# Layer 1's cross attention: the last keys' share moved within a turn, and the convolution's passes set apart

## The chip, the cores and the metric

The kernel runs on one core of one Trainium2 chip. The core has TensorE (PE, matmuls into PSUM), VectorE (DVE), ScalarE (ACT), GpSimd (POOL) and SyncE (SP, which issues most DMAs). Each engine works through its own queue in order and waits for the others by semaphores. The metric is device microseconds of one execution, the median of several runs.

## The reference, cut to what matters

Two layers work on `x` of 64 sequences x 32 places x 256 features. The change lies in layer 1, where a cross attention to 257 context rows per sequence (16 heads of 16 features) is followed by a gated mixer with a convolution over three places:

```python
x = x + xattn(layernorm(x), ctx, ctx, mask)      # 16 heads, 257 keys
...
xpad = jnp.pad(x, ((0, 0), (1, 1), (0, 0)))
t_out = xpad[:, :-2] * conv_w[:, 0] + xpad[:, 1:-1] * conv_w[:, 1] + xpad[:, 2:] * conv_w[:, 2]
return t_out + y_global
...
x = x + moe(layernorm(x))                        # 8 experts, 2 per token, 1 shared
```

All arithmetic is float32 but for a few exact bf16 operands. The output is the final `x`.

## The kernel before

The 2048 rows of `x` lie in four groups of four tiles of 128 rows; a tile is four sequences. Layer 0 runs first and ends near 240 us. Layer 1's cross attention runs from there to about 715 us, then the mixture of experts (`mixture`), with gathers, an expert loop and the final sum.

**Turns and steps.** `cross_attention` (L984) is a software pipeline: turn `i` of 18 handles three tiles at once, `after` (keys), `now` (scores and exponentials) and `before` (transposes and context), with `done` being projected. A turn has four steps `b`, one per sequence of the tile. The order of the work is written out by hand: every engine's queue follows the order of the Python calls. In one step PE sees: the first `ps_t` (four transposes of `before`'s weights), `ps_p` (the projection of `done`, in step 1 alone), `ps_v` (values), the second `ps_t`, the side work's matmuls, `ps_k` (keys), `ps_s` (scores), `ps_le` (step 1 alone) and `ps_o` (context).

DVE sees: the copy `eT` of the first `ps_t`, the reciprocal of the sums (`xsm`), in every second step the two `own` operations, in step 1 the add `x<-ps_p`, the copy `eT` of the second `ps_t`, the side work, and four minima (`CUSTOM_DVE_ANT_0 e<-ps_s,mask`, each with a short read of `xnm`). ACT takes the exponentials after the minima, and copies `v`, keys and transposes. POOL scales the exponentials (`e<-e,xsm`, four a step, after `last`), and does small and side work.

**The last key.** 257 is 256 + 1. The weights of the last key are gathered in `last` by POOL; `spread` (L1157, step 0) makes `lx` from them on POOL; `last_keys` (L1170, step 1) multiplies by a constant on PE (`ps_le`), by the last values on DVE (`lv<-ps_le,vl`) and adds the values' bias on POOL (`lv<-lv,vec`). `own_heads` (L1242), run one step after the context of steps 1 and 3, adds `ps_o` to `lv` on DVE and gives `own`, which `project` uses.

**Banks.** `ps_t` has one PSUM bank (b5), so the second `ps_t` of a step needs the first to be copied. Most of the rest (`ps_p`, `ps_v`, `ps_k`, `ps_le`, and all matmuls of side work) share a ring of two banks, b0 and b1, taken in turn in program order: a matmul waits until the reader of the one before the last is done.

**Side work.** Each step also takes a piece of a generator (`next(side)`, L1353). In turns 0 to 11 it is layer 0's linear part (`linear`: four rounding operations on `big`, `y` and `q` in steps 1 and 2 of turns 1, 5 and 9; two `ps_ff` in turns 2, 6 and 10), the normalisation and the queries of the next group. From turn 12 it is `late_pieces` (L957): mixers of four tiles for groups 0, 1 and 2, a mixer of two tiles for group 3, and three normalisations for the experts. A normalisation puts DVE's `st`, `mv`, `ve`, `half`, `r`, then fourteen small POOL operations (`sq`, `rn`, `off`), then `y` on ACT or DVE, and adds a bias row to `x` on POOL (`x<-x,rows`). `mixer` (L734) then gives `psT` (transposes), `ps_huv`, a scan `sums`, `hub`, `ps_g`, another `hub`, for each half `c` of the features `ps_d` and three passes of the convolution on DVE (`conv`; only the first reads `ps_d`), and `ps_x`, whose transposes bring `conv` back into `x`.

L120 is the line of all matmuls, L123 of all transposes, L108 of all DVE, ACT, POOL and SP operations. The functions below carry the changed lines.

## Time and profile before

| what | value |
|---|---|
| time, median of 3 runs | 962.22 us (961.95 to 964.1) |
| the profiled execution: its own time | 959.8 us |
| the profiled execution: its span | 958.0 us |
| mean granted clock of PE | 0.981 |
| PE busy in the span | 879.9 us (92%) |
| DVE, ACT, POOL busy | 606.9, 455.1, 541.4 us |
| PE busy from 620 to 645 us | 24.17 of 25 us |
| PE busy from 645 to 670 us | 17.93 of 25 us |
| PE busy from 670 to 695 us | 23.86 of 25 us |

Times in the profile are microseconds from the start of the span. A timeline's line has start, duration, engine, line, operation, output<-inputs and shape; in brackets stands the idle time of the engine just before it and who ended that. PE's ends are modelled, and successive matmuls overlap a little, so the text works with the distance from start to start.

### The profile page before, as it was taken

The page shows a single profiled execution, that of the slowest core. Times are in us where ns is not written, and L with a number is a line of the kernel's source. Part 1 is how long each engine was busy: PE and PEld are TensorE (multiplying, and loading weights), DVE is VectorE, ACT ScalarE, POOL GpSimd, SP SyncE. Part 2 cuts the span into 40 slices and gives each one's busy share as a digit, 9 for nine tenths or more (in the row PEclk, how much of TensorE's full clock was granted, in tenths as well). Part 3 has the DMA queues.
Part 4 walks back from the last instruction along what each step waited for, and adds up shares of the span by engine and source line. Part 5 has one row for each costly group of instructions (what it writes and reads, how often), then busy time and mean ns, then how long its engine had stood idle before and what let it go on. Part 6 is the DMA issues. An engine that isn't in the chain of part 4 may idle for free.

```text
span 958.0 us, 21439 instructions
## 1 busy us (share of the span) xinstructions
PE 879.9 (92%) x8005; PEld 607.9 (63%) x8035; DVE 606.9 (63%) x1734; ACT 455.1 (48%) x1163; POOL 541.4 (57%) x1056
## 2 busy tenths in 40 slices
PE   5899899888999999999999999997988999999991
PEld 3466666565456666566666665654757688888881
DVE  6889997797676677676777566877647722111116
ACT  3667677665455555454555466554532212222210
POOL 5779787893684656574755556647513045554420
PEclk9999999999999999999999999999999989999996
DMA  6753335343110111111111003000010337767617
GB/s 184 211 139 101 74 83 138 77 123 105 46 50 7 51 51 51 51 51 51 51 51 51 18 35 95 1 2 23 23 34 23 122 108 246 231 231 236 200 58 263
DMA packets 66073, 89.73 MB, mean 94 GB/s; under 512 B 31504, under 2 KB 49072, under 8 KB 63920
## 3 DMA queue, kind: packets, MB, share of 16 engines
q1 hardware_dynamic: 62128, 77.86, 26.5%
q0 software_dynamic: 3840, 10.49, 3.3%
q8 instruction: 64, 1.05, 0.5%
q14 instruction: 41, 0.34, 0.1%
HBM read 66.30 MB, written 13.63 MB: 83 GB/s over the span
## 4 chain that ended last, share of the span: by engine, by line
PE 50%; DVE 14%; POOL 14%; issue 10%; DMA 6%; ACT 4%; SPq 2%; POOLq 0%; ACTq 0%; DVEq 0%
PE ps_v L120 10%; PE ps_k L120 10%; PE ps_t L123 6%; PE ps_s L120 5%; PE ps_o L120 4%; POOL yg L108 4%; POOL r_rows L1721 3%; PE ps_p L120 3%; PE ps_qk L120 3%; PE ps_sh L120 3%; ACT e L108 3%; DMA r_rows<-og,lv 2%; SPq L108 2%; POOL sq L108 1%; PE ps_q L120 1%
## 5 line engine op out<-in xcount | busy, mean ns | idle before, releaser
L108 ACT ACTIVATE e<-e,xnm 128x257 f32<-128x257 f32 x256 | 127.8, 501 | 52.0 <-DVE xnm L108 46.0
L108 DVE CUSTOM_DVE_ANT_0 e<-ps_s,mask 128x257 f32<-128x257 f32 x256 | 93.4, 420 | 50.1 <-PE ps_s L120 49.3
L120 PE MATMUL ps_k<-ct,w_w_l1x 128*128 128x512 f32 x256 | 122.3, 600 | 1.6 <-ACT yT L108 0.6
L120 PE MATMUL ps_v<-w_w_l1x,ct 128*128 128x256 f32 x512 | 121.9, 381 | 0.0
L108 POOL TENSOR_SCALAR e<-e,xsm 128x256 f32<-128x256 f32 x256 | 121.1, 491 | 0.0
L123 PE MATMUL ps_t<-cst,e 128*128 128x128 f32 x640 | 100.5, 280 | 7.8 <-DVE eT L108 6.9
L108 DVE COPY eT<-ps_t 128x512 f32<-128x512 f32 x128 | 87.9, 687 | 26.8 <-PE ps_t L123 26.7
L120 PEld LDWEIGHTS ps_v<-w_w_l1x,ct 128*128 128x128 f32 x512 | 94.1, 192 | 11.0 <-issue 0.2
L123 PEld LDWEIGHTS ps_t<-cst,e 128*128 128x128 f32 x640 | 74.0, 141 | 35.5 <-issue 14.6
L108 POOL TENSOR_TENSOR x<-x,rows 128x256 f32<-128x256 f32 x96 | 70.5, 751 | 40.0 <-DVE y L108 17.0
L108 ACT ACTIVATE hTr<-ps_h,w 128x256 f32<-128x256 f32 x80 | 33.7, 472 | 124.9 <-issue 97.3
L108 ACT ACTIVATE kT<-ps_k,vec 128x512 f32<-128x512 f32 x64 | 44.2, 691 | 100.5 <-PE ps_k L120 100.3
L108 DVE TENSOR_TENSOR og<-ps_o,b 128x512 f32<-128x512 f32 x20 | 13.8, 690 | 116.0 <-PE ps_o L120 113.3
L1721 POOL DMA_INDIRECT r_rows<-og,lv x40 | 39.5, 987 | 70.2 <-DVE og L108 59.9
L108 ACT ACTIVATE kb<-kT,cst 128x256 f32<-128x256 f32 x160 | 70.9, 513 | 4.1 <-POOL kT L108 4.1
L120 PE MATMUL ps_h<-ygT,w 128*128 128x256 f32 x320 | 72.4, 379 | 0.0
L120 PE MATMUL ps_o<-w,hTr 128*128 128x256 f32 x320 | 72.2, 379 | 0.0
L120 PEld LDWEIGHTS ps_k<-ct,w_w_l1x 128*128 128x128 f32 x256 | 44.5, 190 | 41.6 <-issue 35.3
L120 PEld LDWEIGHTS ps_o<-w,hTr 128*128 128x128 f32 x320 | 60.8, 190 | 8.3
L108 ACT COPY v<-ps_v 128x512 f32<-128x512 f32 x80 | 46.7, 584 | 37.5 <-PE ps_v L120 37.1
L120 PEld LDWEIGHTS ps_h<-ygT,w 128*128 128x128 f32 x320 | 59.3, 190 | 7.3
L108 POOL TENSOR_TENSOR last<-e,xsm 128x4 f32<-128x4 f32 x64 | 12.9, 202 | 89.9 <-DVE xsm L108 89.9
(197 smaller groups left out, 1728.2 us busy)
## 6 DMA issues: line engine op xcount, KB each, us to landing
ct<-in_ctxT SPq DMA_DIRECT2D x16, 1024.0 KB
w<-in_ew SPq DMA_DIRECT2D x20, 514.0 KB
w<-in_ew SPq DMA_DIRECT2D x20, 512.0 KB
far<-part SPq DMA_DIRECT2D x64, 128.0 KB
v_rows<-v SPq DMA_DIRECT2D x16, 256.0 KB
vb<-v_rows SPq DMA_DIRECT2D x64, 64.0 KB
r<-r_rows SPq DMA_DIRECT2D x8, 512.0 KB
b<-in_eb SPq DMA_DIRECT2D x20, 128.0 KB
```

The lines of the kernel that those rows point to most:

```text
L108: ins = getattr(self.engine, name)(*args, **kw)
L120: return kept(nc.tensor.matmul(ps, **args))
L123: return kept(nc.tensor.transpose(ps, src, eye))
L1721: wrote = nc.gpsimd.indirect_dma_start(out=r_rows, out_offset=bass.IndirectOffsetOnAxis(ap=write_i[:, at : at + 1], axis=0), in_=o[:, i, : ...
```

## The change

`last_keys(before)` moves within step 1 from behind the scores to a place between the second `turned` and the side work. The second and third pass of the convolution are no longer issued at once: they are put in a list, `vector_later`, and `vector_steps` takes one of them out behind the scores of a step (behind the four minima, ahead of the next step's first `eT` copy) and one ahead of `values` and the second `turned` of a step (ahead of the second `eT` copy). In mixers of two tiles (`n == 2`) both are taken out at once.

```diff
+    vector_later = []
+
+    def vector_steps(n=1):
+        for _ in range(min(n, len(vector_later))):
+            vector_later.pop(0)()
+
...
             vector.scalar_tensor_tensor(got, yT[:, c, :], tap(1), ps, ALU.mult, ALU.add)
-            vector.scalar_tensor_tensor(
-                dst[:, :, 1:S], src[:, :, 0 : S - 1], tap(0), dst[:, :, 1:S], ALU.mult, ALU.add
-            )
-            vector.scalar_tensor_tensor(
-                dst[:, :, 0 : S - 1], src[:, :, 1:S], tap(2), dst[:, :, 0 : S - 1], ALU.mult, ALU.add
-            )
+            vector_later.append(
+                lambda dst=dst, src=src, by=tap(0): vector.scalar_tensor_tensor(
+                    dst[:, :, 1:S], src[:, :, 0 : S - 1], by, dst[:, :, 1:S], ALU.mult, ALU.add
+                )
+            )
+            vector_later.append(
+                lambda dst=dst, src=src, by=tap(2): vector.scalar_tensor_tensor(
+                    dst[:, :, 0 : S - 1], src[:, :, 1:S], by, dst[:, :, 0 : S - 1], ALU.mult, ALU.add
+                )
+            )
+            if n == 2:
+                vector_steps(2)
             conv.append(got)
...
                 if before is not None:
+                    vector_steps()
                     v = values(before, b)
                     turned(before, b, 1, eT)
                     if b == 0:
                         spread(before)
+                    if b == 1:
+                        last_keys(before)
                 next(side, None)
...
                     weights = scores(now, b)
+                vector_steps()
                 if before is not None:
-                    if b == 1:
-                        last_keys(before)
                     own_heads = context(before, b, eT, v)
```

## Prediction

> **What bounds the kernel now.** I read the page first, for the engine that sets the pace; then TensorE's waits between 240 and 715 us, where layer 1's attention runs; then the timelines of TensorE, VectorE and GpSimd around each wait.

> ```profile
> PE 879.9 (92%) x8005; PEld 607.9 (63%) x8035; DVE 606.9 (63%) x1734; ACT 455.1 (48%) x1163; POOL 541.4 (57%) x1056
> PE   5899899888999999999999999997988999999991
> PEclk9999999999999999999999999999999989999996
> ```

> TensorE (PE) is full in nearly every slice from the 11th to the 27th; the 28th (647 to 670 us) is not. So in the attention a change gains or loses only what it does to PE's own waits:

> ```profile
> PE ps_t L123 <- DVE eT L108: 6.9, 6, 2.9
> PE psT L123 <- DVE conv L108: 5.8, 5, 2.2
> PE ps_le L120 <- DVE hub L108: 0.7, 1, 0.7
> ```

> Total us, times, longest. All three end on VectorE (DVE): the copy of transposed weights (eT), the first convolution pass that empties the bank ps_d, and hub. Where the large ones stand, on PE:

> ```profile
> 389.12 0.66 PE L123 MATMUL ps_t<-cst,e 128*128 128x128 f32 x4 [0.86 <-DVE eT L108]
> ...
> 646.61 0.63 PE L123 MATMUL ps_t<-cst,e 128*128 128x128 f32 x4 [0.91 <-POOL rn L108]
> ...
> 649.11 1.12 PE L120 MATMUL ps_g<-hub,gw 64*128 64x512 f32 x2 [0.90 <-DVE x L108]
> ...
> 663.47 0.66 PE L123 MATMUL ps_t<-cst,e 128*128 128x128 f32 x4 [2.90 <-DVE eT L108]
> ...
> 667.50 0.66 PE L123 MATMUL psT<-cst,y 128*128 128x128 f32 x4 [2.07 <-DVE conv L108]
> ...
> 670.62 2.65 PE L120 MATMUL ps_v<-w_w_l1x,ct 128*128 128x256 f32 x8
> ...
> 696.68 0.66 PE L123 MATMUL psT<-cst,y 128*128 128x128 f32 x4 [2.20 <-DVE conv L108]
> 698.10 0.66 PE L123 MATMUL psT<-cst,y 128*128 128x128 f32 x4 [0.76 <-DVE conv L108]
> ```

> The reader is to see that 7.9 us of waits stand between 660 and 698. The reason is on DVE, in the same stretch:

> ```profile
> 657.29 2.12 DVE L108 SCALAR_TENSOR_TENSOR conv<-yT,vec,conv 128x496 f32<-128x496 f32 x2
> ...
> 662.40 0.42 DVE L108 TENSOR_TENSOR lv<-ps_le,vl 128x256 f32<-128x256 f32 x1
> 662.74 0.68 DVE L108 COPY eT<-ps_t 128x512 f32<-128x512 f32 x1
> ...
> 665.46 0.35 DVE L108 SCALAR_TENSOR_TENSOR own<-ps_o,cst,lv 128x128 f32<-128x128 f32 x1 [1.55 <-POOL lv L108]
> ...
> 694.91 0.35 DVE L108 SCALAR_TENSOR_TENSOR own<-ps_o,cst,lv 128x128 f32<-128x128 f32 x1 [2.86 <-POOL lv L108]
> ```

> and behind it on GpSimd (POOL):

> ```profile
> 661.19 0.19 POOL L108 TENSOR_TENSOR sq<-r 128x2 f32<-128x2 f32 x1 [0.51 <-DVE r L108]
> ...
> 664.81 0.61 POOL L108 TENSOR_TENSOR lv<-lv,vec 128x256 f32<-128x256 f32 x1
> ```

> Two convolution passes and lv hold up the eT copy. Then own waits for POOL's lv, which stood behind a normalisation's fourteen small steps (sq ... off), and the eT copy and the convolution's first pass queue behind own.

> **Part one: last_keys moves ahead of the side work.** Nothing is added; in 16 turns the ps_le matmuls (0.58 us from start to start), DVE's lv (0.42, the next instruction 0.34 later) and POOL's lv (0.61) move up. No DMA moves, so SP's queue is as before. On POOL, lv goes ahead of the bias adds and the sq steps, which start up to 0.6 us later; their readers on ScalarE come microseconds later. PE could now wait for POOL's lx: the tightest turn has lx done at 270.55, while the new place is at 271.30. Cost nothing; if that cover went, one turn would pay part of lx's 1.2 us.

> The banks do change. The ring has two: ps_p, ps_v, then ps_le takes the bank of ps_p and the next matmul that of ps_v. By the rows, x<-ps_p is done before that in 14 turns; in the two others (457 and 655 us) the same wait was already paid by the matmul that followed. ScalarE's copy of v ends about 0.85 us after the second ps_t starts; the new user comes at 1.01. Again nothing, with a cover of 0.1. The third user of the ring waits for lv.

> - Rounding turns (3: lv at 276, 381, 486). DVE has no gap between the eT copy and the minima, because of four rounding operations. lv now delays the minima by 0.38, then the exponentials, the reciprocal and the whole next step, where PE already waits (0.86 in the row at 389). 3 x 0.38 = +1.1.
> - Output turns of the linear layer (3: around 301, 406, 511). ps_k is the third user: its place is 299.65, lv ends at 299.85, release 0.06 later. 3 x 0.26 = +0.8.
> - Turns that transpose or normalise (8): the second psT waits 0.16 for lv, but ps_k waits anyway until ScalarE has emptied the first. The eT copy of the next step comes 0.2 later against a slack of 0.64 before PE needs it. 0.
> - The turn at 592: ps_le waits 0.68 for hub, as third user. Now ps_huv is second and nothing waits for hub until ps_v, at 593.75 against hub's new end of 593.27. -0.7.
> - The last two turns (657, 689): POOL's lv ends near 659 and 687 instead of 665.42 and 694.87, so own waits no longer. Counted below.

> **Part two: the passes.** Per channel half the first pass stays; the second goes behind the four minima and ahead of the next eT copy, the third ahead of the other eT copy. Six halves of three four-tile mixers are touched. In the two-tile mixers both passes run at once, in the old order: 0. A pass takes 0.74 us alone and 1.08 beside POOL's bias adds; I take 0.75 for the second and 0.75 to 0.95 for the third, which starts when POOL begins to scale e. Five on the path at the far ends would be 5 x 0.33 = 1.7, which goes into the range.

> - 604 to 623: minima waited for PE there (0.62 idle), so the passes were free; now the eT copy at 609.84 starts 0.75 late, PE pays 0.15. One turn on, the eT copy, lv and the transposes ps_x stand in a row and ps_g pays 0.34. +0.5.
> - 637: the eT copy is late by 0.1. +0.1.
> - 642 to 649: the worst place. The passes ran while DVE waited for ScalarE's hub (they ended at 641.07, the scan began at 641.23). Now the second stands between minima and eT copy: 0.72 on the wait of 0.91. The third follows own, at 648.45, and ps_x needs it: ps_g starts at 650.65 instead of 649.11. So with the two lines above PE is 1.5 late here. +0.9.
> - 655 to 663: without the two passes ahead (2.12) the minima start at 661.0 as before, though their inputs come 1.5 later. No lv, one pass: the eT copy ends at 663.9, PE goes on at 663.95. From 1.5 late to 0.5 late: -1.1.
> - 663 to 667.5: own does not wait (1.55), the third pass costs 0.75; the first pass of the other half ends at 666.75 instead of 667.45. From 0.5 late to 0.7 early: -1.2.
> - 667.5 to 675: the minima come 2.1 earlier. The granted clock reads 0.50 from 670 to 672 here: ps_o, ps_t and ps_v took 1.08, 1.12 and 2.65 us against 0.65, 0.66 and 1.89 in other turns, 1.65 more. With the waits cut from 5.0 to 3.0 us I take this as gone: -1.5; ps_x then waits 0.3 for a third pass: +0.3.
> - 689 to 698: own starts 2.9 earlier; what limits is then ps_t and ps_d themselves, and psT goes on 1.9 earlier: -1.9.

> Sum: 1.1 + 0.8 - 0.7 + 0.5 + 0.1 + 0.9 - 1.1 - 1.2 - 1.5 + 0.3 - 1.9 = -2.7 us. After 698 the chain runs through PE into the experts' loop, whose period does not depend on this, so the shift stays. The profiled execution took 959.8 (span 958.0); it would be 957.1. The median of the runs is 962.22, 2.4 above it; the same shift gives 959.5.

> [...] The row: the clock halves at 668.7 after waits of 2.90 and 2.07 us, neither longer. [...]

> **The rivals.**
> 1. *The slow clock stays.* For it: 3 us of waits remain within 6, and other drops stand in this trace (the clock is 0.50 from 765 to 770). Against: two waits of 0.9 within 3 us at 646 brought none. -2.7 + 1.5 = -1.2: 961.0.
> 2. *Slower: the passes stand ahead of the eT copies.* Each of six second passes adds its 0.75 to ps_t's wait, as I see it only at 646. For it: PE takes the second ps_t only when the one bank ps_t is copied, and the passes had idle time to hide in. Against: at 611 and 637 the copy has 0.6 us of slack. Four more such places cost 4 x 0.6 = 2.4, and the step at 655 then gains nothing (+1.1): -2.7 + 3.5 = +0.8; with passes at 1.08 (+1.7) +2.5: 964.7. It decides as soon as the eT copies of 610 to 672 end more than 0.5 after their ps_t's turn.
> 3. *Larger gain.* The rounding and output turns cost nothing (DVE catches up), and the place at 646 neither: -2.7 - 1.9 - 0.9 = -5.5: 956.7.
> 4. *Nothing to see:* gains at the end paid back in the tail, whose slow clock (764 to 774) can begin earlier. 962.

> **How the numbers follow.** The sum 0.40, rival 1 0.20, rival 2 0.18, rival 3 0.14, rival 4 0.08. A measurement of this kernel tells 0.2% (1.9 us) from no change: faster is under 960.3, slower above 964.1. Of the sum's case, which I place between 957.5 and 961, 0.34 lies under 960.3, of rival 1 0.05, all of rival 3: 0.53 faster. Rival 2 gives 0.14 slower, rival 4 0.02, another 0.02 for what I don't see: 0.18. The rest, 0.29, is the same. The range leaves out one in ten at each end: from 955.5 (rival 3 and a little) to 964.8 (rival 2).

> **What would show it.** Right: no wait of own for POOL's lv at the end of the attention; ps_t's 2.90 falls to about 2.0, psT's 2.07 to 1.0, 2.20 and 0.76 to under 1 each; ps_le's wait for hub gone; ps_t's waits near 284, 389 and 494 up by 0.4; ps_k waiting 0.26 for lv in three turns; ps_t near 647 and ps_g near 650 later than before. Wrong: ps_t waits of 0.7 or more near 611, 637 or 672, ps_le waiting for lx, or a half clock at 668.

## The result, and the profile after

The changed kernel takes 959.07 us (median of 20 runs), the kernel before 961.44 us in the runs beside them: a ratio of 0.998 with a 95% interval of 0.9966 to 0.9995. The medians differ by 2.4 us; the ratio makes it 1.9 us less (0.5 to 3.3). The prediction said 959.5 within 955.5 to 964.8, faster with a chance of 0.53. The profiled execution took 955.96 us (span 954.2, mean granted clock 0.982).

The page of the changed kernel, the lines that answer to those of before:

```profile
PE 881.3 (92%) x8005; PEld 604.6 (63%) x8035; DVE 606.3 (64%) x1734; ACT 453.0 (47%) x1163; POOL 543.8 (57%) x1056
PE   5999999889899999999999999997998999999991
PEclk9999999999999999999999999999999989999996
```

At this grain little changes: PE is still full everywhere from the 11th slice on but in the 28th. PE's waits from 240 to 715 us, total us, times, longest:

```profile
PE ps_t L123 <- DVE eT L108: 7.7, 7, 2.4
...
PE psT L123 <- DVE conv L108: 1.7, 4, 0.8
PE ps_t L123 <- DVE xsm L108: 1.6, 1, 1.6
PE ps_x L123 <- DVE conv L108: 0.6, 1, 0.6
PE ps_g L120 <- DVE x L108: 0.5, 2, 0.3
```

Two of the three waits that the prediction began with have changed as it said: psT's wait for the convolution fell from 5.8 to 1.7, and the wait of ps_le for hub is gone. The wait for eT did not fall: its longest piece did (2.9 to 2.4), but the three rounding turns give it back. Where they stand on PE:

```profile
387.65 0.66 PE L123 MATMUL ps_t<-cst,e 128*128 128x128 f32 x4 [1.22 <-DVE eT L108]
...
647.22 0.63 PE L123 MATMUL ps_t<-cst,e 128*128 128x128 f32 x4 [1.56 <-DVE xsm L108]
...
648.51 0.98 PE L123 MATMUL ps_x<-cst,conv 128*128 128x128 f32 x7 [0.56 <-DVE conv L108]
649.84 1.12 PE L120 MATMUL ps_g<-hub,gw 64*128 64x512 f32 x2 [0.35 <-DVE x L108]
...
663.87 1.06 PE L123 MATMUL ps_t<-cst,e 128*128 128x128 f32 x4 [2.43 <-DVE eT L108]
664.72 1.92 PE L120 MATMUL ps_d<-hub,gow 96*128 96x512 f32 x2
666.43 1.71 PE L123 MATMUL psT<-cst,y 128*128 128x128 f32 x8
...
693.56 0.66 PE L123 MATMUL psT<-cst,y 128*128 128x128 f32 x4 [0.18 <-DVE conv L108]
694.97 0.66 PE L123 MATMUL psT<-cst,y 128*128 128x128 f32 x4 [0.76 <-DVE conv L108]
```

And on DVE in the two last turns, where own used to wait for POOL's lv (1.55 and 2.86 us before):

```profile
663.13 0.68 DVE L108 COPY eT<-ps_t 128x512 f32<-128x512 f32 x1
...
663.90 0.32 DVE L108 SCALAR_TENSOR_TENSOR own<-ps_o,cst,lv 128x128 f32<-128x128 f32 x1
...
691.16 0.34 DVE L108 SCALAR_TENSOR_TENSOR own<-ps_o,cst,lv 128x128 f32<-128x128 f32 x1
```

Own now waits for nothing in either place, because POOL adds the values' bias before the normalisation's small steps:

```profile
657.81 0.61 POOL L108 TENSOR_TENSOR lv<-lv,vec 128x256 f32<-128x256 f32 x1
...
661.27 0.19 POOL L108 TENSOR_TENSOR sq<-r 128x2 f32<-128x2 f32 x1
```

**Stage by stage.** Two spans can't be compared directly. The first ps_v of turn 1 starts at 262.04 us before and at 259.21 after, though nothing ahead of it was changed; over all 14 profiles of this study it lies between 258.14 and 264.10. So the attention is cut at starts of PE's groups and each piece is compared by itself (us; the last column is the prediction's sum over the same piece; turns are counted from their first ps_v):

| piece, from start to start on PE | before | after | difference | predicted |
| --- | --- | --- | --- | --- |
| turn 1's first ps_v to turn 13's | 315.82 | 318.89 | +3.07 | +1.9 |
| turn 13 | 31.60 | 31.05 | -0.55 | -0.7 |
| turn 14 | 34.36 | 34.62 | +0.26 | +0.6 |
| turn 15 to the second ps_t of step 2 | 19.65 | 20.10 | +0.45 | -0.2 |
| from there to the scores ps_s | 4.61 | 4.20 | -0.41 | -1.2 |
| from there to turn 16 | 11.08 | 9.99 | -1.09 | -1.2 |
| turn 16 to the second psT behind ps_d | 18.94 | 16.91 | -2.03 | -1.9 |
| sum | 436.06 | 435.76 | -0.30 | -2.7 |

Ahead of the last turns the change costs 3.2 us, in the last turns it gains 3.5. The profiled attention is 0.3 shorter, the timed runs 2.4; the points below come back to the rest. The spans differ by 3.85 us: 2.83 ahead of the table's pieces, 0.30 in them and 0.72 behind them (259.93 against 259.21 from the second psT behind ps_d to the end).

### The profile page after: what moved, and what is told of

It is laid out like the page before. It is cut to its first block, busy times and chain, and to the rows that moved or that the text cites. A ratio compares the mean times of both kernels' runs of the same rounds, so it can differ in the third digit from the quotient of the medians.

```text
span 954.2 us, 21439 instructions
## 1 busy us (share of the span) xinstructions
PE 881.3 (92%) x8005; PEld 604.6 (63%) x8035; DVE 606.3 (64%) x1734; ACT 453.0 (47%) x1163; POOL 543.8 (57%) x1056
## 4 chain that ended last, share of the span: by engine, by line
PE 54%; DVE 15%; POOL 11%; issue 10%; DMA 5%; ACT 4%; SPq 0%; POOLq 0%; ACTq 0%; DVEq 0%
PE ps_k L120 10%; PE ps_v L120 10%; PE ps_t L123 6%; PE ps_s L120 5%; PE ps_o L120 4%; POOL yg L108 4%; PE ps_qk L120 3%; PE ps_p L120 3%; POOL r_rows L1735 3%; PE ps_sh L120 3%; DMA r_rows<-og,lv 2%; ACT e L108 2%; DVE x L108 2%; PE ps_q L120 1%; PE psT L123 1%
## 5 line engine op out<-in xcount | busy, mean ns | idle before, releaser
L108 ACT ACTIVATE e<-e,xnm 128x257 f32<-128x257 f32 x256 | 127.2, 499 | 50.7 <-DVE xnm L108 44.8
L108 DVE CUSTOM_DVE_ANT_0 e<-ps_s,mask 128x257 f32<-128x257 f32 x256 | 93.5, 421 | 57.6 <-PE ps_s L120 57.2
L120 PE MATMUL ps_k<-ct,w_w_l1x 128*128 128x512 f32 x256 | 124.4, 609 | 0.9 <-ACT qT L108 0.5
L108 POOL TENSOR_SCALAR e<-e,xsm 128x256 f32<-128x256 f32 x256 | 122.2, 496 | 0.0
L120 PE MATMUL ps_v<-w_w_l1x,ct 128*128 128x256 f32 x512 | 121.1, 379 | 0.0
L123 PE MATMUL ps_t<-cst,e 128*128 128x128 f32 x640 | 100.6, 280 | 9.2 <-DVE eT L108 7.7
L108 DVE COPY eT<-ps_t 128x512 f32<-128x512 f32 x128 | 87.7, 685 | 21.1 <-PE ps_t L123 21.0
L120 PEld LDWEIGHTS ps_v<-w_w_l1x,ct 128*128 128x128 f32 x512 | 93.4, 190 | 10.9 <-issue 0.2
L123 PEld LDWEIGHTS ps_t<-cst,e 128*128 128x128 f32 x640 | 73.6, 141 | 37.7 <-issue 15.0
L108 ACT ACTIVATE kT<-ps_k,vec 128x512 f32<-128x512 f32 x64 | 44.1, 688 | 108.4 <-PE ps_k L120 108.1
L108 ACT ACTIVATE hTr<-ps_h,w 128x256 f32<-128x256 f32 x80 | 33.5, 470 | 124.3 <-issue 94.9
L108 POOL TENSOR_TENSOR last<-e,xsm 128x4 f32<-128x4 f32 x64 | 14.1, 220 | 135.4 <-DVE xsm L108 135.3
L108 POOL TENSOR_TENSOR x<-x,rows 128x256 f32<-128x256 f32 x96 | 69.5, 740 | 33.2 <-DVE y L108 17.7
L108 DVE TENSOR_TENSOR og<-ps_o,b 128x512 f32<-128x512 f32 x20 | 13.8, 691 | 116.2 <-PE ps_o L120 113.5
L108 ACT ACTIVATE kb<-kT,cst 128x256 f32<-128x256 f32 x160 | 70.6, 510 | 4.5 <-POOL kT L108 4.5
L120 PEld LDWEIGHTS ps_k<-ct,w_w_l1x 128*128 128x128 f32 x256 | 44.8, 191 | 43.9 <-issue 36.0
L120 PE MATMUL ps_h<-ygT,w 128*128 128x256 f32 x320 | 72.4, 379 | 0.0
L120 PE MATMUL ps_o<-w,hTr 128*128 128x256 f32 x320 | 72.2, 379 | 0.0
L120 PEld LDWEIGHTS ps_o<-w,hTr 128*128 128x128 f32 x320 | 60.8, 190 | 8.3
L120 PEld LDWEIGHTS ps_h<-ygT,w 128*128 128x128 f32 x320 | 59.3, 190 | 7.3
L108 POOL DMA_INDIRECT yg<-y_rows,lv x40 | 39.0, 974 | 42.3 <-DVE lv L108 30.4
```

The lines of the kernel that those rows point to most:

```text
L108: ins = getattr(self.engine, name)(*args, **kw)
L120: return kept(nc.tensor.matmul(ps, **args))
L123: return kept(nc.tensor.transpose(ps, src, eye))
```

## Experiments

Each kernel is read in two ways: by the pieces of the table, and by its ratio to the kernel before.

### A: one part alone

Last keys early in every turn, but all three passes at once everywhere:

```diff
-            if n == 2:
-                vector_steps(2)
+            vector_steps(2)
```

> last_keys ahead of the side work in all turns, the convolution's passes at once as before. Measure: PE's timeline from the first ps_v of turn 1 to the first ps_v of turn 13 (315.82 us before, 318.89 in the changed kernel) and from there to the second psT after the last mixer's ps_d of the attention (120.24 before, 116.87 changed). Theory A (the early turns pay for the moved ps_le, the late turns gain because own no longer waits for POOL's lv): early +3.1 as in the changed kernel, late -4 (hub -0.5, 655 to 675 us -1.5, the last turn -2), total -1 us against before. Theory B (the gain is the convolution's): early 0 within 0.3, late above -1.

Measured: 0.9984 (0.9967 to 1.0002). Turns 13 to 16 take 31.06, 34.61, 34.09 and 16.92 us, against 31.60, 34.36, 35.34 and 18.94 before. The early turns pay as in the changed kernel: turns 2 to 4 and 6 to 12 agree with it within 0.02. (Turn 1 was disturbed by a wait from the end of layer 0, and turn 5 by a stretch from 394.6 to 398.0 in which the granted clock reads 0.50; such a stretch is called halved below.) Turns 15 and 16 of this profile hold a halved stretch too, at 671.

The passes apart, last keys at their old place:

```diff
-                    if b == 1:
-                        last_keys(before)
                 next(side, None)
...
                 if before is not None:
+                    if b == 1:
+                        last_keys(before)
                     own_heads = context(before, b, eT, v)
```

> The convolution's second and third passes set apart, last_keys behind the scores as before. Theory A: early 0; late +1 (ps_t near 646 waits 0.6 more, ps_g 0.4 more, and own still waits for POOL's lv near 665 and 694), total +1 us. Theory B: late -3, total -3 us.

Measured: 1.0028 (1.001 to 1.0046), so this part alone makes the kernel slower. Turn 1 to turn 13 takes 315.75, as before. Turn 14 takes 34.78 (+0.42), and the place that the prediction called the worst is there alone too:

```profile
647.80 0.63 PE L123 MATMUL ps_t<-cst,e 128*128 128x128 f32 x4 [1.56 <-DVE xsm L108]
```

Turns 15 and 16 take 36.29 and 19.26, 1.3 more than before, and hold three halved stretches (at 664, 678 and 698) where before had one.

So most of the late gain comes from the last keys. The passes alone lose in the first two mixers (0.42 in turn 14, 0.78 in turn 15 up to its second ps_v) and gain in the third: from that ps_v to the second ps_t of step 2 they take 10.17 against 10.74 before, while the last keys alone take 10.99 there.

### B: the last keys only where they gain

```diff
-                    if b == 1:
+                    if b == 1 and i > 12:
                         last_keys(before)
                 next(side, None)
...
                 if before is not None:
+                    if b == 1 and not (i > 12):
+                        last_keys(before)
                     own_heads = context(before, b, eT, v)
```

> The changed kernel, but last_keys moves only in turns 13 to 16 and stays behind the scores in turns 1 to 12. Theory A: early 0 (315.8), late -3.4 as in the changed kernel, total -3.4 us against before and 3.1 better than the changed kernel's attention. Theory B (the early 3.1 us are an accident of that run): early +3 or scattered, total as the changed kernel.

Measured: 0.9951 (0.9932 to 0.9971), and turns 2 to 12 are those of before within 0.04 each (turn 1 took 28.34 against 27.32). Turns 13 to 16 take 117.91 against 120.24: 2.3 less, where 3.4 was expected, with two halved stretches in them (at 667 and 677). The next kernel takes turn 14 out as well, and lets the first two mixers run their passes at once:

```diff
-            if n == 2:
+            if n == 2 or g < 2:
                 vector_steps(2)
...
-                    if b == 1:
+                    if b == 1 and i in (13, 15, 16):
                         last_keys(before)
...
                 if before is not None:
+                    if b == 1 and not (i in (13, 15, 16)):
+                        last_keys(before)
```

> last_keys moves only in turns 13, 15 and 16, and the passes are set apart only in the third mixer (655 to 675 us), at once in the first two. Theory A: early 0, nothing lost near 609 to 649, late -5.6 (hub -0.5, 655 to 675 -3.2, last turn -1.9): -5.6 us against before, faster than the changed kernel. Theory B: no better than the changed kernel, because two of three mixers lose the spread passes.

Measured: 955.62 us, 0.9934 (0.9909 to 0.9958) of before. The pieces: 315.81, 31.06, 34.35, 32.59 (turn 15), 16.91; the attention takes 430.72, 5.3 less than before. No halved stretch fell on it in this profile, while one of 1.65 us fell on that of before, so part of the 5.3 is luck of the two profiles; the ratio rests on all runs. This version beats both kernels and is the base of what follows.

### C: the price of an early turn

The prediction gave the turns that neither round nor put out a price of 0. They paid (the condition behind the scores changes with the one shown, here and below):

```diff
-                    if b == 1 and i in (13, 15, 16):
+                    if b == 1 and i in (3, 4, 7, 8, 11, 12, 13, 15, 16):
```

> The best version so far (last keys early in turns 13, 15 and 16 alone, passes apart in the third mixer alone), with the last keys early also in turns 3, 4, 7, 8, 11 and 12, which neither round nor put out. From the first ps_v of turn 1 to that of turn 13 the best version took 315.81 us. The prediction's step (0 per such turn) gives 315.8 again. The theory now (each moved ps_le costs PE 0.1 to 0.2, because ps_k's weights no longer come ahead) gives 316.5 to 316.9. If the price were made only by the rounding and output turns together with others, something between.

Measured: 316.62 against the base's 315.81; the six turns pay 0.14, 0.13, 0.16, 0.09, 0.16 and 0.19, the others nothing. (The ratio to before is 0.9944, 0.9916 to 0.9972.) To find the cause, the same six turns with ps_le behind ps_k in place of ahead of it:

```diff
                     keys(after, b)
+                if before is not None and b == 1 and i in (3, 4, 7, 8, 11, 12):
+                    last_keys(before)
                 if now is not None:
                     weights = scores(now, b)
```

> As the run before, but in the six turns 3, 4, 7, 8, 11 and 12 the last keys stand behind the keys and ahead of the scores, so that ps_k follows the second ps_t directly and its weights can come ahead. If weight loads are the price, the stretch from turn 1 to turn 13 is within 0.2 of 315.8. If the price is lv's earlier place on DVE or POOL, or the third user of the ring, it stays 0.6 to 1.1 longer.

Measured: 315.80, each of the six turns within 0.01 of the base. So the price belongs to the place between the second ps_t and ps_k. PE's weight loads (PEld) show what changes there. In the kernel before:

```profile
351.63 0.57 PEld L123 LDWEIGHTS ps_t<-cst,e 128*128 128x128 f32 x4
352.25 0.30 PEld L120 LDWEIGHTS ps_k<-ct,w_w_l1x 128*128 128x128 f32 x2
```

In the run with the six turns early, the same turn:

```profile
351.98 0.57 PEld L123 LDWEIGHTS ps_t<-cst,e 128*128 128x128 f32 x4
352.72 0.20 PEld L120 LDWEIGHTS ps_le<-lx,of 128*64 128x64 f32 x4 [0.17 <-POOL sq L108]
353.30 0.30 PEld L120 LDWEIGHTS ps_k<-ct,w_w_l1x 128*128 128x128 f32 x2 [0.39 <-ACT v L108]
```

Before, ps_k's first load starts at 352.25, before its matmul at 352.28 and 0.62 after ps_t's first load. Early, ps_le's load comes 0.74 after it, and the load of ps_k starts with its matmul (both 353.30), no longer ahead of it. On PE, from the second ps_t to ps_o, the step takes 3.65 (352.19 to 355.84) against 3.53 before (351.84 to 355.37). With ps_le behind ps_k it is 3.52:

```profile
353.10 0.60 PE L123 MATMUL ps_t<-cst,e 128*128 128x128 f32 x4
353.54 1.95 PE L120 MATMUL ps_k<-ct,w_w_l1x 128*128 128x512 f32 x4
355.42 0.65 PE L120 MATMUL ps_le<-lx,of 128*64 128x256 f32 x4
356.00 0.69 PE L120 MATMUL ps_s<-kT,qb 32*64 32x257 f32 x16
356.62 0.65 PE L120 MATMUL ps_o<-eT,v 128*32 128x64 f32 x32
```

The move also changes which bank each group takes (ps_k then takes ps_v's, whose reader is the copy of v). The rows speak against the bank's release as the price. On PE, before and with the six turns early:

```profile
351.84 0.60 PE L123 MATMUL ps_t<-cst,e 128*128 128x128 f32 x4
352.28 1.96 PE L120 MATMUL ps_k<-ct,w_w_l1x 128*128 128x512 f32 x4
```

```profile
352.19 0.60 PE L123 MATMUL ps_t<-cst,e 128*128 128x128 f32 x4
352.72 0.65 PE L120 MATMUL ps_le<-lx,of 128*64 128x256 f32 x4
353.30 1.98 PE L120 MATMUL ps_k<-ct,w_w_l1x 128*128 128x512 f32 x4
```

The copy of v ends at 353.04, 0.26 ahead of ps_k, and ps_k follows ps_le after 0.58, the distance that ps_le also has to ps_o behind the scores. Most of the price lies ahead of ps_le: it starts 0.53 after ps_t, where ps_k started 0.44 after it. The distance is 0.53 as well in turns 3, 7, 11 and 12, where the add x, which frees ps_le's bank, had ended some 0.88 earlier. Why the change from the transposes to ps_le takes 0.09 longer is not shown; behind the scores ps_le's load starts with its matmul too, and costs nothing there. The earlier place of lv on DVE and POOL is not the price: it is still ahead of the minima here.

The rounding turns:

```diff
-                    if b == 1 and i in (13, 15, 16):
+                    if b == 1 and i in (1, 5, 9, 13, 15, 16):
```

> The best version with the last keys early also in the rounding turns 1, 5 and 9. By the prediction's step (lv ahead of the minima, 0.38 each) the stretch from turn 1 to turn 13 is 1.1 longer than 315.81, so 316.9; with the weight loads on top of it, 0.1 to 0.2 more per turn, 317.2 to 317.6.

Measured: 317.19 against 315.81, by turn +0.23, +0.59 and +0.58. (Ratio 0.9951, 0.9924 to 0.9977.) This is the chain that the prediction described: lv ahead of the minima, and a wait at the next step's ps_t of 1.24 against 0.86, plus the price of the place on PE. What remains of the changed kernel's 3.07 is 0.28 for each output turn (predicted 0.26); no run sets these apart, so they are read from the changed kernel's rows below.

### D: the passes in the first two mixers, and turn 16

The base with the mixers exchanged: passes apart in the first two, at once in the third.

```diff
-            if n == 2 or g < 2:
+            if n == 2 or g == 2:
                 vector_steps(2)
```

> Last keys as in the best version (early in turns 13, 15, 16), but the convolution's passes apart in the first and second mixer and together in the third: the opposite of the best version. From the first ps_v of turn 13 to the last psT behind turn 16's ps_d the best version took 114.91 us (31.06 + 34.35 + 32.59 + 16.91). By the prediction's steps the first two mixers pay 0.5 + 0.1 + 0.9, and the third loses some 0.7 by its passes together (the wait ahead of the second ps_t of step 2 was 3.05 there against 2.45), so about 117.1, plus up to 1.7 if a halved stretch falls on it. If setting the passes apart costs nothing once the last keys are early, 115.6 without a halved stretch, and the loss of the version with passes apart alone (1.0028 of before) has another cause.

Measured: turn 13 31.06, turn 14 34.77 (+0.42), turn 15 up to the second ps_t 20.76 against 19.33. Of these 1.43, 0.78 come in the turn's first step (9.69 against 8.91, around the ps_x that waits for the third pass), and 0.62 by the longer wait ahead of the second ps_t in the third mixer (3.07 against 2.45):

```profile
644.51 0.98 PE L123 MATMUL ps_x<-cst,conv 128*128 128x128 f32 x7 [0.56 <-DVE conv L108]
...
660.53 1.11 PE L123 MATMUL ps_t<-cst,e 128*128 128x128 f32 x4 [3.07 <-DVE eT L108]
```

So in the first two mixers the passes apart cost 1.2 (0.42 + 0.78), in the third they gain 0.6. The whole late stretch took 119.72, more than expected: one halved stretch followed this wait, at 660.5, and another, at 674.1, the matmuls ps_r that start at 671. The pieces behind the wait, in which both lie, are 3.0 longer than the base's. Ratio to before 0.9964 (0.9942 to 0.9986).

The base with turn 16's last keys at their old place:

```diff
-                    if b == 1 and i in (13, 15, 16):
+                    if b == 1 and i in (13, 15):
```

> The best version with the last keys at their old place in turn 16. The prediction's step for 689 to 698 (own waits 2.9 for POOL's lv, then ps_d's bank) gives a way from turn 16's first ps_v to the last psT 1.9 longer than the best version's 16.91, so 18.8, and a wait of about 2.2 on psT for conv. If POOL's lv were on time anyway, now that the rest runs earlier, 16.9.

Measured: 18.94 for turn 16, exactly that of before, against 16.91; the wait of 2.20 is back:

```profile
694.09 0.66 PE L123 MATMUL psT<-cst,y 128*128 128x128 f32 x4 [2.20 <-DVE conv L108]
695.51 0.66 PE L123 MATMUL psT<-cst,y 128*128 128x128 f32 x4 [0.76 <-DVE conv L108]
696.00 5.29 PE L120 MATMUL ps_sh<-yT,w_shared 128*128 128x512 f32 x8
```

The eight ps_sh behind it took 5.29 instead of 3.60: a halved stretch followed this wait too. Ratio 0.996 (0.9933 to 0.9987).

### E: the slow clock

The prediction counted 1.5 us on a halved clock that would go when the waits shrink. In the changed kernel it did not go; it stands at 664.0 to 667.4, right behind the 2.43 us wait, in the rows above (1.06, 1.92 and 1.71 for groups that took 0.66, 1.02 and 0.60 + 0.66 at full clock). The first test fills that wait in the changed kernel with two matmuls that nobody reads:

```diff
                     v = values(before, b)
+                    if i == 15 and b == 2:
+                        ps_f = psum.tile([P, 2, D], F32, tag="b3", name="ps_f")
+                        for _ in range(2):
+                            mm(
+                                ps_f.rearrange("p a d -> p (a d)"),
+                                lhsT=w[:, 2, 0, 0:P],
+                                rhs=before["ct"][:, 0, 0:2, :].rearrange("p b k -> p (b k)"),
+                                start=True,
+                                stop=True,
+                            )
                     turned(before, b, 1, eT)
```

> The changed kernel with two matmuls of 128x512 that nobody reads (about 1.9 us together) put on PE ahead of the second ps_t of step 2 in turn 15, into the 2.43 us wait at 663.87. If that wait is what makes the granted clock halve just behind it (664 to 667.4 in the changed kernel's profile, 668.7 to 672.2 in the one of before), no halved stretch stands between 660 and 680, and the time is below the changed kernel's by up to 1.5. If halved stretches fall there by chance of the run, the profile may show one again and the time is that of the changed kernel within 0.5 (959.1 against a before of 961.4).

Measured: no halved stretch between 660 and 680, as the first theory has it, and the piece from ps_t to ps_s takes 3.27 instead of 4.20. The time is 960.87 us, 0.9972 (0.9948 to 0.9995) of before: no gain over the changed kernel that could be told. The same on the base:

> The best version with the same two unread matmuls in the wait ahead of the second ps_t of step 2 in turn 15. In the ten profiles so far the granted clock changes only at whole multiples of 3.413 us from each other, with a phase that differs from run to run; near 660 us a halved stretch followed each of the stretches in which PE was busy for 0.39 or less, and none in which it was busy for 0.46 or more. If that is the rule, no halved stretch can follow this wait, whatever the phase, and the profile shows none between 662 and 690; on the median it is worth at most the share of phases that would be hit (about half) times 0.8 to 1.7, so 954.8 to 955.6 if the best version is 955.6 against a before of 961.3; this difference is near what five rounds can tell.

Measured: 954.89 us, 0.9932 (0.9906 to 0.9958), the same as the base. No halved stretch follows the filled wait. But the second half of the expectation failed: one stands at 674.0, behind another stretch. The windows below show it (us, then busy time and count of PE, PEld, DVE, ACT, POOL, and the granted clock):

```profile
660.41:663.82 3.41, 3.10 (x10) 1.44 (x11) 3.38 (x12) 2.52 (x9) 2.58 (x11) 1.00 0.00 0
670.56:673.98 3.42, 3.07 (x26) 2.84 (x27) 1.97 (x5) 0.00 (x0) 1.74 (x4) 1.00 0.02 5
673.98:677.39 3.41, 3.41 (x56) 2.18 (x55) 2.29 (x16) 1.95 (x6) 1.74 (x9) 0.50 0.00 0
```

PE was busy for 3.07 of the 3.42 us ahead of it, but for 1.81 of them with the sixteen ps_r, each with an output of 8 columns only. Not counting ps_r it was busy for 0.37 of the stretch. With ps_r left out, a reading made after this result and resting on six stretches of the same kind, the profiles agree here; no run tested why ps_r should not count. In each, the halved stretches start whole multiples of 3.413 us apart (668.74 and 733.60 in the kernel before, 663.97 and 728.83 in the changed kernel: 19 times 3.413 in both), on a grid whose phase (its place against the kernel's own work) differs from profile to profile. The grid stretch ahead of the halved one in the kernel before, and the halved one:

```profile
665.31:668.73 3.42, 1.35 (x26) 0.68 (x24) 3.17 (x6) 1.13 (x3) 2.09 (x6) 1.00 0.00 0
668.73:672.14 3.41, 3.41 (x47) 2.98 (x41) 3.41 (x14) 2.46 (x9) 1.41 (x2) 0.50 0.00 0
```

In the changed kernel:

```profile
660.57:663.99 3.42, 0.99 (x6) 0.54 (x5) 3.42 (x13) 2.37 (x9) 2.65 (x10) 1.00 0.00 0
663.99:667.40 3.41, 3.41 (x10) 1.96 (x10) 2.54 (x6) 0.18 (x1) 3.08 (x11) 0.50 0.00 0
```

And in the run with the rounding turns early, which has the same 2.4 us wait, here cut in two by the grid, and no halved stretch behind it:

```profile
658.60:662.01 3.41, 1.55 (x8) 1.02 (x6) 3.38 (x12) 1.68 (x7) 2.86 (x8) 1.00 0.02 6
662.01:665.43 3.42, 2.12 (x11) 1.35 (x12) 3.38 (x8) 1.46 (x4) 2.87 (x11) 1.00 0.00 0
```

Over the grid stretches from 643 to 700 us of the 14 profiles, 17 have PE busy, ps_r not counted, for 0.43 or less of their length: each was followed by a halved one. Of all others, from 0.44 up, one was (0.47). Over the rest of the time from 20 to 750 us, 25 more were busy for 0.43 or less, and each was followed by a halved one (0.23 at 214.8 in the kernel before, 0.26 at 725.4 in the changed kernel). From 0.44 up the profiles do not agree: from 240 to 643 us, 10 of the 19 grid stretches with a share between 0.44 and 0.60 were followed by a halved one, nine of them near 248 us with a share of 0.48 or 0.49, and one (0.56) behind the 1.22 us wait of a rounding turn, at 391 us with the last keys alone. In the changed kernel the stretch at 244.1, busy for 1.65 of 3.41 us, was followed by a halved one; in the kernel before the one at 248.9, busy for as long, was not. And in every profile the clock halves near 760 us behind grid stretches that PE's records fill throughout (from 764.3 in the kernel before, from 763.0 in the changed kernel). So from 0.44 up PE's busy share does not tell here whether a halved stretch follows. Each theory of the first test is borne out in part: neither run with the fill shows a halved stretch right behind the filled wait; of the 12 profiles without it, ten show one that starts between 660 and 672, and in the two others, the base and the run with the rounding turns early, the grid cuts the wait (PE busy for 1.69 and 1.96 us in the base's two stretches, for 1.55 and 2.12 in the other's, above).

Last, the kernel before once more, for what a second profile of the same code changes:

> The kernel before, unchanged, profiled a second time. Theory: what differs between profiles of the same code is where layer 0 ends (258 to 264 us at the first ps_v of turn 1 in the profiles so far, though none of these kernels touches layer 0) and the phase of the 3.413 us grid on which the granted clock halves. Then every stretch that keeps the full clock repeats: turn 1 to turn 13 in 315.8 within 0.1, turn 13 in 31.6, turn 14 in 34.36, turn 15 up to the second ps_t of step 2 in 19.65, turn 16 to its last psT in 18.94, all within 0.1. Worked out over all phases from the profile of before, with halving wherever PE is busy (ps_r not counted) for less than 0.44 of a grid stretch, a halved stretch follows near 660 to 668 in about 9 of 10 phases, and near 696 in about 7 of 10. If the halved stretches came from the code alone, they would stand where they stood: at 668.7 of that profile, and none near 696. A rival for the whole: that the differences of a few tenths that stages show between kernels are scatter; then this second profile differs from the first by as much.

Measured: 315.79, 31.60, 34.35, 19.70 and 18.96 against 315.82, 31.60, 34.36, 19.65 and 18.94; turn 1 starts at 261.00 instead of 262.04. So differences of 0.1 in the pieces mean something, while those of spans do not. The halved stretch fell at 667.7, near where it was, behind a grid stretch that was busy for 0.39, and none at 696. This phase was too close to the first to tell the grid from the code; that rests on the other profiles.

## Why the prediction was right, point by point

The forecast time was met within 0.5 us. Its own sum was not: over the pieces that it summed, the profiles show -0.3 where it has -2.7. The sign and the places were largely right, the number had luck. Of the 2.4 us between the two sums, 1.2 lies in the early turns, 0.65 in turn 15 up to the wait at 663, and 0.8 on the halved clock behind that wait.

- **Last keys, turns that transpose or normalise: "0".** The step that failed. It gave the bank's release a cover of 0.1 and looked at DVE; the price came on PE itself, where ps_le starts 0.53 after ps_t instead of the 0.44 of the group that followed before. The bank was not it: in turn 4 the copy of v had released ps_v's bank 0.26 before its new user. Six turns pay 0.08 to 0.21, 0.84 together, and none of it with ps_le behind ps_k. Together with the rounding turns this is why the early turns cost 3.07 rather than 1.9.
- **Rounding turns: 3 x 0.38 = 1.1.** Right mechanism; 1.4 measured (0.26, 0.55 and 0.58), the price on PE being on top.
- **Output turns: 3 x 0.26 = 0.8.** 3 x 0.28, but the number is partly luck. The wait of ps_k for lv is there (lv ends at 297.29, ps_k starts at 297.35 in the first of them), and is worth 0.16: from ps_ff to ps_k 0.62 instead of 0.46. Another 0.09 is the price of ps_le's place behind ps_t, which the prediction did not have.
- **Hub at 592: -0.7.** -0.55, and the wait of 0.68 is gone. The changed order puts ps_le early at its own price.
- **604 to 637: +0.6.** +0.26 in turn 14. With only the last keys early it is +0.25 as well, with only the passes +0.42: the two overlap.
- **642 to 649: +0.9.** +0.78, in the rows named (ps_t near 647, ps_x, ps_g near 650).
- **655 to 663: -1.1.** Only -0.33 (+0.45 with the 0.78 before it). The wait ahead of ps_t fell as forecast in kind, 2.90 to 2.43 where the list of signs said about 2.0. Two things held it up. ps_le now stands ahead of ps_d and waits 0.43 for the add x: with the last keys alone, the stretch from the second ps_v of the turn is 0.25 longer than before. And 0.96 of the 2.12 us that left DVE's queue came back: half and r, two small operations of the normalisation ahead of the minima, took 0.65 each instead of 0.17. They used to start when POOL's bias add had ended and now run beside it, as the rows of before and of the changed kernel show:

```profile
657.03 3.65 POOL L108 TENSOR_TENSOR x<-x,rows 128x256 f32<-128x256 f32 x4
660.74 0.17 DVE L108 TENSOR_SCALAR half<-ve 128x2 int32<-128x2 int32 x1
660.94 0.17 DVE L108 TENSOR_SCALAR r<-half 128x2 int32<-128x2 int32 x1
```

```profile
658.38 2.78 POOL L108 TENSOR_TENSOR x<-x,rows 128x256 f32<-128x256 f32 x4
659.87 0.65 DVE L108 TENSOR_SCALAR half<-ve 128x2 int32<-128x2 int32 x1
660.55 0.65 DVE L108 TENSOR_SCALAR r<-half 128x2 int32<-128x2 int32 x1
```

The second profile of the kernel before has 0.17 for each again (at 659.71 and 659.91).
- **663 to 667.5: -1.2.** Right at full clock: the base version needs 3.27 from ps_t to ps_s against 4.61. In the changed kernel's profile the halved clock took 0.93 of it back (4.20).
- **667.5 to 675: -1.2 with the slow clock gone.** -1.09. The piece itself lost its halved stretch, but that had only moved ahead by 4.7 us. So in this profile rival 1, "the slow clock stays", came true. What the prediction treated as one outcome differs from profile to profile. As an estimate from the PE rows of the two profiles, with a halved stretch taken to follow wherever PE is busy for less than 0.44 of a grid stretch, one starts between 655 and 672 in 0.91 of all phases before and in 0.6 after, and it costs 1.65 before and 0.93 after: 0.91 x 1.65 - 0.6 x 0.93 = 0.9 to be counted on, not 1.5.
- **689 to 698: -1.9.** -2.03, and putting turn 16's last keys back takes exactly this away.
- **The rivals.** Rival 2 (slower) has its mechanism at one place, 647, and with the passes alone it is what happens: 1.0028. In the changed kernel the last keys outweigh it. Rival 3 named the base version's gain, without the rounding turns, the output turns and the place at 646: it gave 5.5 us less, and the version that leaves these out takes 5.7 less by the medians (955.62 against 961.33). Rival 4 (gains paid back in the tail) did not come: the time from the second psT behind turn 16's ps_d to the end is 259.93 before and 259.21 after. Over the 14 profiles it is 258.0 to 259.3 in the seven where the clock near 765 is halved for 6.8 us, and 259.9 to 263.7 in the seven where it is for 10.2, so the tail is in part a draw too.

**What stays open.** The pieces sum to -0.3, the timed runs to -2.4 by the medians and -1.9 by the ratio, whose interval reaches down to -0.5. Part may lie in the draws of the clock, of which a profile shows only one. Behind the wait at 663 the two profiles differ by 0.7, where 0.9 was to be counted on. And the 2.2 us wait in turn 16, which the change removes, was followed by a halved stretch in two of the four profiles that had it, for 1.7 us (5.29 against 3.60): 0.8 on average that the profile of before does not show. Together that would be -0.3 - 0.2 - 0.8 = -1.3, inside the interval; it is argued, not shown. The end of layer 0, which the change does not touch, differs by 6 us between profiles; a median over 20 runs may not remove all of that.

The prediction took the halved stretch as gone because the two waits together fall from 5.0 to 3.0 us. That sum is not what the profiles follow. In the changed kernel one grid stretch, from 660.57 to 663.99, held the whole wait of 2.43 us, PE was busy for 0.99 of its 3.42 us, and a halved one followed; in the run with the rounding turns early the grid cut the same wait in two, and none followed. Between 643 and 700 us halved stretches followed stretches in which PE was busy for 0.12 to 0.47, ps_r not counted.

## What to carry to other kernels

- A move that takes a wait away in three turns was paid for in thirteen. Asking turn by turn and mixer by mixer where each part gains made 0.2% into 0.66%. Behind one of the longer waits of the rounding turns (1.22 us, in the profile with the last keys alone) the granted clock read 0.50 from 394.6 to 398.0, and ps_k took 3.39 us instead of 1.98.
- A small matmul group put behind the transposes cost PE 0.08 to 0.21 us a turn here, though nobody waited for its data; the same group one place later cost nothing. Cost a move by what it separates, on PE too.
- Work that comes earlier runs beside other work. Here 0.96 of the 2.12 us that left DVE's queue near 657 went to two small operations that came to run beside one of POOL's.
- Compare profiles by pieces from start to start, not by spans, and count a slow clock as a chance: between 660 and 672 us a halved stretch started in ten of the 12 profiles without the fill.
